# Four graph layers on one core: a comparison of the dilation on 2-byte operands in pairs of batches, and the second batch's transposes at the head of layer 2

## The chip, the core and the metric

The kernel runs on one core of one Trainium2 chip, as one program. The core has a matrix engine (TensorE, PE in the profile; its weight loads are listed apart as PEld), a vector engine (VectorE, DVE), a scalar engine (ScalarE, ACT), GpSimd (POOL) and a queue for transfers (SyncE, SP). Each engine works through its own list of instructions strictly in the order that the build gave it, and waits on semaphores for the others. The metric is the device time of one execution in microseconds (us); before the change the median of three runs is 2661.71 us.

## What is computed

Sixteen graphs of 1024 nodes with 128 features go through four layers; after each, the layer's output is added to its input and a layer norm is taken.

```python
x = _layernorm(x + _L0_gnn_ref(x, adj, ...))            # attention with a gate
x = _layernorm(x + _L1_gnn_ref(x, adj, nodemask, ...))  # dilation, then 3 x SAGE with batch norm
x = _layernorm(x + _L2_gnn_ref(x, adj, ...))            # attention, three gates
x = _layernorm(x + _L3_gnn_ref(x, adj, ...))            # GCN with the undilated adjacency
```

The dilation, which opens layer 1, runs over the rows of each graph's adjacency one after the other, and every row sees what the rows before it removed:

```python
row = jnp.take(carry, n, axis=0); nbi = row.astype(jnp.int32)
num = jnp.sum(nbi)
sf = jnp.where(num > T_DIL, (num + K_DIL - 1) // K_DIL, 1)
rank = jnp.cumsum(nbi)
rm = row & (rank % sf == 0)          # at most the middle and the last neighbour
carry = carry.at[n].set(row & ~rm); carry = carry.at[:, n].set(carry[:, n] & ~rm)
```

Layer 2 begins with the end of layer 1: `xc @ Wl + bl` on three hidden tensors, the residual and the layer norm. Then come `h = x W^T + b`, `G = A h`, and the attention, in which each score is the product of a row of `G` and a row of `h`.

## The kernel before, in words

The function `fast_kernel` builds the whole program. Tiles have 128 partitions; a graph is 8 x 8 blocks of 128 x 128. The loops are Python generators that are advanced in turns (`take_turns`, L811, `in_rounds`, L815, where a yielded number says how many rounds a stream pauses). From that program order a scheduler of the framework makes each engine's final list; an instruction marked with `keep_in_program_order` stays where the program put it.

**The dilation** (L1034 to L1193) handles a block of 128 rows k at a time, for two groups g of eight batches: 16 steps (k, g). Three generators share the work:

- `prepare` (L1047): for each half group of four batches, 32 products of `Y` blocks with step matrices make prefix counts `s0` in PSUM (L1068), and DVE multiplies them by the masked block into `sk`, float16, tile [128, 8 batches, 128] (L1070). For the last two blocks of rows (`with_last`) a tile `last` is made too (L1076).
- `fixed_point` (L1079): the rows of a block depend on each other, so the threshold of each row is found by iteration, `EVALS[k]` times (2, 3, 4, 7, 7, 3, 3, 9 for k = 0 to 7). One evaluation is: `thr = ti | 1` (L1091, int32, 8 numbers per partition), for the last two blocks `even` (L1094); the comparison `mid = (sk == thr)` over 1024 elements with an fp8 result (L1096); eight products of one column each that count `mid` into `pd` (L1099; with `last` eight more, L1101); and `ti = pd + v1m` (L1103). The final `mid` is removed from `Y` by xor (L1112), and a chain of small operations ends in `negc`, `posc` and `wid` (L1116 to L1129), which the removals of that step need. L1109 and L1112 read the final `mid` as 4-byte words, so it has to lie batch by batch.
- `removal` (L1132), once for each batch: 8 products (L1141, L1143), two ACT operations into `q` (L1144), on DVE `keep` (L1147) and an `and` into the rows (L1148), 9 products (L1151 to L1155), and one ACT operation that writes the columns back (L1156).

`take_turns` (L1180) lets the fixed point of step i alternate with the removals of step i - 1, among which the preparation of the same group's next block is spread. So one evaluation, one removal, and now and then half a preparation follow each other in DVE's list.

**The head of layer 2** is `before` (L1633) for batches 0 and 1 (L1819), ahead of all attention. For each batch GpSimd makes `yb`, the bias row times the node mask (L1639, one buffer); 24 products make `p` (L1644); DVE adds `yb` (L1660), adds the residual (L1664), and `normed` (L787) takes the layer norm, with its power on GpSimd (L745) and its last step on ACT (L801, eight pieces). `turned` (L754) transposes `xn` on PE (L759), ACT copies it to `xT` (L1669), and `products` (L762) with ACT copies makes `hT` (L1673) and `G` (L1677). `attention` (L1687) of batch 0 starts with a score product (L1706) and its masked minimum on DVE (L1711).

Of the kernel before, what the change touches and what calls it, by code (L numbers as in the profile page):

```python
# [10 lines left out]
F16 = mybir.dt.float16  # L11
F32R = mybir.dt.float32r
BF16 = mybir.dt.bfloat16
I32 = mybir.dt.int32
I8 = mybir.dt.int8
FP8 = mybir.dt.float8e4
AF = mybir.ActivationFunctionType
OP = mybir.AluOpType
# [4 lines left out]
P = 128  # L23
# [4 lines left out]
EVALS = 2, 3, 4, 7, 7, 3, 3, 9  # L28
GB = 8
QB = 4  # L30
# [609 lines left out]
def fast_kernel(ctx: ExitStack, tc: tile.TileContext, t: dict, out: bass.AP, flag: bass.AP):  # L640

    nc = tc.nc
    B, N, D = t["x"].shape
    NT = N // P
# [6 lines left out]
    identf = consts.tile([P, P], F32, name="identf")  # L651
# [18 lines left out]
    mf = consts.tile([P, BT], F32, name="mf")  # L670
# [57 lines left out]
    def tiles3(ap):  # L728
        return ap.rearrange("p (t d) -> p t d", d=P)

    def per_row(v):

        return v[:, :, None].to_broadcast([P, NT, P])

    def per_col(v):
        return v[:, None, :].to_broadcast([P, NT, P])
# [14 lines left out]
            p = psum.tile([P, 512], F32, name="ph", tag=tag)  # L751
            yield p, slice(h * 512, (h + 1) * 512), range(h * 4, h * 4 + 4)

    def turned(psum, src, tag="h"):  # L754

        for p, c, blocks in halves(psum, tag):
            for i, k in enumerate(blocks):
                s = src[:, k, :] if len(src.shape) == 3 else src[:, k * P:(k + 1) * P]
                nc.tensor.transpose(p[:, i * P:(i + 1) * P], s, identf)  # L759
            yield p, c, slice(blocks[0], blocks[-1] + 1)  # L760

    def products(psum, *pairs, tag="h"):  # L762
# [102 lines left out]
    onec = consts.tile([P, 1], BF16, name="onec")  # L865
# [26 lines left out]
    ps_h = ending.enter_context(tc.tile_pool(name="l0_ph", bufs=2, space=PSUM, reuse_waits="tile"))  # L892

    with tc.tile_pool(name="l0_raw", bufs=1, side="right") as raw:
# [4 lines left out]
        p = ps_h.tile([P, P], F32, name="wtr", tag="h")  # L899
# [3 lines left out]
        p = ps_h.tile([P, P], F32, name="wtr", tag="h")  # L903
# [3 lines left out]
        p = ps_h.tile([P, 1], F32, name="wtr", tag="h")  # L907
# [126 lines left out]
    with ExitStack() as ph:  # L1034
        sb = ph.enter_context(tc.tile_pool(name="dl_sb", bufs=2, side="right", reuse_waits="tile"))
        tiny = ph.enter_context(tc.tile_pool(name="dl_small", bufs=2, side="right", reuse_waits="tile"))
# [7 lines left out]
        def per_member(v):  # L1044
            return v[:, :, None].to_broadcast([P, v.shape[1], P])

        def prepare(st, k, g):  # L1047

            ks = slice(k * P, (k + 1) * P)
            st.with_last = k >= NT - 2  # L1050
            st.sk = sb.tile([P, GB, P], F16, name="sk")
            st.v1m = tiny.tile([P, GB], F32, name="v1m")
            st.l1 = tiny.tile([P, GB], F32, name="l1")
            if st.with_last:
                st.last = sb.tile([P, GB, P], FP8, name="last")
            for q in range(GB // QB):
                qs = slice(q * QB, q * QB + QB)
                b0 = g * GB + q * QB
                gs = slice(b0, b0 + QB)
                Yg = Yq[b0 // QB]  # L1060
                uY = sb.tile([P, QB, P], FP8, name="uY")
                nc.vector.tensor_tensor(words(uY), words(Yg[:, :, k, ks]),
                                        words(upper8)[:, None, :].to_broadcast([P, QB, P // 4]), op=OP.bitwise_and)
                s0 = ps_b.tile([P, QB, P], F32, name="s0")
                for i in range(QB):
                    for kb in range(NT):
                        m = step0 if kb == k else twos[:, :P if kb < k else 1]
                        nc.tensor.matmul(s0[:, i, :m.shape[1]], Y[b0 + i][:, kb, ks], m, start=(kb == 0), stop=(kb == NT - 1))  # L1068
                l1 = st.l1[:, qs]
                nc.vector.tensor_tensor(st.sk[:, qs, :], s0, uY, op=OP.mult)  # L1070
                nc.vector.scalar_tensor_tensor(l1, s0[:, :, 0], -1.0, off[:, k, gs], op0=OP.add, op1=OP.add)
                if not st.with_last:

                    nc.vector.tensor_tensor(past[:, k, gs], l1, s0[:, :, P - 1], op=OP.subtract)
                if st.with_last:
                    nc.vector.tensor_tensor(st.last[:, qs, :], st.sk[:, qs, :], per_member(l1), op=OP.is_equal, saturate=False)  # L1076
                yield

        def fixed_point(st, k, g):  # L1079

            ks = slice(k * P, (k + 1) * P)
            gs = slice(g * GB, (g + 1) * GB)
            st.negc = negc = tiny.tile([P, GB], F32, name="negc")
            st.wid = wid = tiny.tile([P, GB], F32, name="wid")
            v1m, l1 = st.v1m, st.l1
            nc.vector.tensor_scalar(v1m, l1, 0.5, -0.5, op0=OP.mult, op1=OP.add)
            ti = tiny.tile([P, GB], I32, name="ti")
            nc.vector.tensor_copy(ti, v1m)
            for e in range(EVALS[k]):
                thr = tiny.tile([P, GB], I32, name="thr")  # L1090
                nc.vector.tensor_scalar(thr, ti, 1, None, op0=OP.bitwise_or)  # L1091
                if st.with_last:
                    even = tiny.tile([P, GB], BF16, name="even")
                    nc.vector.tensor_tensor(even, thr, ti, op=OP.is_equal)  # L1094
                mid = sb.tile([P, GB, P], FP8, name="mid")
                nc.vector.tensor_tensor(mid, st.sk, per_member(thr), op=OP.is_equal, saturate=False)  # L1096
                pd = ps_d.tile([P, GB], F32, name="pd")
                for i in range(GB):
                    nc.tensor.matmul(pd[:, i:i + 1], mid[:, i, :], onec, start=True, stop=not st.with_last)  # L1099
                    if st.with_last:  # L1100
                        nc.tensor.matmul(pd[:, i:i + 1], st.last[:, i, :], even[:, i:i + 1], start=False, stop=True)  # L1101
                tn = tiny.tile([P, GB], I32, name="ti")
                nc.vector.tensor_tensor(tn, pd, v1m, op=OP.add)  # L1103
                prev, ti = ti, tn
                yield
            nc.vector.tensor_tensor(bad[:, 0, k, gs], ti, prev, op=OP.not_equal)
            if st.with_last:
                nc.vector.tensor_tensor(st.last, st.last, per_member(even), op=OP.mult, saturate=False)
                nc.vector.tensor_tensor(words(mid), words(mid), words(st.last), op=OP.bitwise_or)  # L1109
            for q in range(GB // QB):  # L1110
                yw = words(Yq[g * GB // QB + q][:, :, k, ks])
                nc.vector.tensor_tensor(yw, yw, words(mid[:, q * QB:(q + 1) * QB]), op=OP.bitwise_xor)  # L1112


            v = tiny.tile([P, GB], F32, name="v")
            nc.vector.tensor_sub(v, l1, ti)  # L1116
            hw = tiny.tile([P, GB], F32, name="hw")
            nc.vector.tensor_tensor(hw, thr, prev, op=OP.is_equal)
            nc.vector.tensor_sub(negc, hw, v)
            nc.vector.scalar_tensor_tensor(hw, v, 0.5, hw, op0=OP.mult, op1=OP.mult)  # L1120
            nc.vector.tensor_sub(negc, negc, hw)
            st.posc = posc = tiny.tile([P, GB], F32, name="posc")
            nc.vector.scalar_tensor_tensor(posc, v, 2.0, negc, op0=OP.mult, op1=OP.add)
            en = tiny.tile([P, GB], F32, name="en")
            mk = mok[:, g * GB * NT + k:(g + 1) * GB * NT:NT]
            nc.vector.scalar_tensor_tensor(en, v, 10.5, mk, op0=OP.is_gt, op1=OP.mult)
            nc.vector.tensor_tensor(bad[:, 1, k, gs], en, mk, op=OP.not_equal)
            nc.vector.scalar_tensor_tensor(hw, hw, 1.0, en, op0=OP.add, op1=OP.mult)
            nc.vector.tensor_scalar(wid, hw, -1.0, None, op0=OP.add)  # L1129
            yield  # L1130
# [127 lines left out]
    with ExitStack() as ph:  # L1258
# [6 lines left out]
        ps_h = ph.enter_context(tc.tile_pool(name="l1_ph", bufs=4, space=PSUM, reuse_waits="tile"))  # L1265
# [290 lines left out]
    with ExitStack() as ph:  # L1556
# [3 lines left out]
        ps_h = ph.enter_context(tc.tile_pool(name="l2_ph", bufs=2, space=PSUM, reuse_waits="tile"))  # L1560
# [72 lines left out]
        def before(s, b):  # L1633
# [2 lines left out]
                l2.load(s, b)  # L1636
            yield 2
            yb = rows("yT")
            nc.gpsimd.tensor_tensor(yb, per_row(mf[:, b * NT:(b + 1) * NT]), per_col(blrow), op=OP.mult)  # L1639

            def summed(p, blocks, ls):
                for i, j in enumerate(blocks):
# [13 lines left out]
            for p, blocks in turns:  # L1656
                if b >= 2:
                    summed(p, blocks, range(3))
                k = slice(blocks[0], blocks[-1] + 1)
                nc.vector.tensor_add(yn[:, k, :], tiles3(p), yb[:, k, :])  # L1660
            yield 2

            for k in spans(b < 2):
                nc.vector.tensor_add(s.xn[:, k, :], s.xn[:, k, :], yn[:, k, :])  # L1664
            normed(small, s.xn, b < 2)
            yield 6
            s.xT = wide("xT", 2)
            for p, c, _ in turned(ps_h, s.xn):
                nc.scalar.copy(s.xT[:, c], p)  # L1669
            yield 1  # L1670
            s.hT = wide("hT", 2)
# [210 lines left out]
```

## Time and profile before

| what | value |
|---|---|
| median of three runs | 2661.71 us (2660.23 to 2662.22) |
| the profiled execution: its own time | 2657.81 us |
| its span in the trace | 2656.1 us |
| mean granted TensorE clock | 0.984 |
| busy share of the span | PE 94%, PEld 69%, DVE 79%, ACT 74%, POOL 13% |
| first and last comparison of the dilation (L1096) | 622.0 and 963.8 us |
| removals of the last step (7, 1) | 968.4 to about 991 us |
| head of layer 2: last transfer of layer 1's `h2T` issued, first masked minimum of the attention | 1620.3 and 1659.6 us |
| 1700 to 2500 us (layers 2 and 3 in rounds) | PE busy 98 to 99% of each 100 us |

The profile is one execution. Start times are counted from the start of its span. In rows of groups, the number behind the bar is the total busy time in us, the next is the mean duration of one instruction in ns, then the idle time of the engine just before, and what ended it. In a table of windows each engine has its busy time in that stretch and in brackets its instructions; PEclk is the granted share of the full TensorE clock. In a timeline the first number is the start, the second the length in us, and what stands in square brackets is the engine's idle time ahead of that instruction with the instruction that ended it.

### The profile page before, as it was taken

The numbers are of one execution on the slowest core, as the hardware profiler recorded it, in microseconds if no ns is written. First come the engines' busy times: TensorE is split into PE (matmuls) and PEld (weight loads), VectorE is DVE, ScalarE is ACT, GpSimd is POOL, SyncE is SP. The second block draws the span as 40 slices with busy tenths as digits, with TensorE's granted clock in tenths as the row PEclk, the third lists the DMA queues.
The fourth block names the chain that finished last, engine by engine and source line by source line (L and its number), as shares of the span: only waits on it lengthen the run. The fifth ranks groups of instructions, "written<-read, shape, count | busy, mean of one in ns | idle before, by whom it ended". The sixth has DMA issues, their size and how long they took to land.

```text
span 2656.1 us, 44982 instructions
## 1 busy us (share of the span) xinstructions
PE 2509.0 (94%) x16580; PEld 1838.7 (69%) x16584; DVE 2106.4 (79%) x5832; ACT 1957.0 (74%) x3141; POOL 356.3 (13%) x316
## 2 busy tenths in 40 slices
PE   7999999997888869999999998999999999999987
PEld 5777777675666648888888896566666666666655
DVE  5888888887899877777788875777888787887786
ACT  7898898886888866667656534777777777777774
POOL 0001111013000001111122133011111111111001
PEclk9999999998999989999999998999999999999998
DMA  5555555530000052224467582111222111111100
GB/s 195 177 171 176 167 167 183 168 113 21 2 3 2 2 214 96 96 96 146 156 241 249 198 291 105 40 48 65 74 87 70 64 64 64 64 64 64 48 25 26
DMA packets 110103, 285.72 MB, mean 108 GB/s; under 512 B 12080, under 2 KB 53168, under 8 KB 102704
## 3 DMA queue, kind: packets, MB, share of 16 engines
q1 hardware_dynamic: 88832, 197.17, 22.1%
q0 software_dynamic: 21040, 85.57, 9.1%
q8 instruction: 133, 2.18, 0.3%
q14 instruction: 98, 0.80, 0.1%
HBM read 202.85 MB, written 79.82 MB: 106 GB/s over the span
## 4 chain that ended last, share of the span: by engine, by line
PE 53%; DVE 19%; ACT 13%; issue 5%; POOL 4%; DMA 2%; POOLq 0%; ACTq 0%; DVEq 0%; SPq 0%
PE acc L1306 9%; PE ph L1628 8%; PE acc L1694 6%; PE ph L1440 5%; PE ph L759 3%; PE ph L1644 3%; PE acc L973 2%; PE pmm L1706 2%; PE pmm L724 2%; PE ph L1615 2%; ACT em L985 2%; PE ph L766 2%; ACT xn L801 2%; DVE mid L1096 2%; DVE keep L1147 2%
## 5 line engine op out<-in xcount | busy, mean ns | idle before, releaser
L973 PEld LDWEIGHTS acc<-hs,em 128*128 128x128 f32 x2048 | 250.2, 193 | 38.2 <-issue 27.0
L973 PE MATMUL acc<-hs,em 128*128 128x128 f32 x2048 | 270.6, 280 | 0.9 <-DVE hs L989 0.7
L1694 PE MATMUL acc<-ex,hs 128*128 128x512 f32 x512 | 250.3, 599 | 6.2 <-DVE hs L1721 4.1
L724 PE MATMUL pmm<-xT,G 128*128 128x512 f32 x512 | 251.4, 604 | 1.4 <-DVE mx L983 0.7
L801 ACT ACTIVATE xn<-xn,ln_nb,ln_rstd 128x128 f32<-128x128 f32 x512 | 204.8, 480 | 55.3 <-DVE ln_nb L799 55.3
L1306 PE MATMUL acc<-a,hi 128*128 128x512 f32 x768 | 235.0, 398 | 3.0 <-ACT hi L1272 3.0
L1306 PE MATMUL acc<-a,lo 128*128 128x512 f32 x768 | 228.3, 392 | 3.1 <-DVE lo L1273 3.1
L745 POOL TENSOR_TENSOR ln_rstd<-ln_rstd,mhalf 128x8 f32<-128x8 f32 (+1 forms) x69 | 107.9, 1564 | 806.1 <-DVE ln_rstd L742 452.2
L1714 ACT ACTIVATE ex<-em,mn 128x1024 f32<-128x1024 f32 x128 | 146.6, 1145 | 89.2 <-DVE mn L1711 85.9
L983 DVE CUSTOM_DVE_ANT_0 em<-pmm,msk 128x1024 f32<-128x1024 f32 x128 | 155.9, 1218 | 35.5 <-PE pmm L724 33.2
L985 ACT ACTIVATE em<-em,mx 128x1024 f32<-128x1024 f32 x128 | 146.0, 1141 | 48.0 <-DVE mx L983 46.4
L1706 PE MATMUL pmm<-G,hT 128*128 128x512 f32 (+3 forms) x416 | 171.4, 520 | 0.1
L1306 PEld LDWEIGHTS acc<-a,lo 128*128 128x128 f32 x768 | 142.9, 188 | 34.0 <-DVE lo L1273 4.5
L1306 PEld LDWEIGHTS acc<-a,hi 128*128 128x128 f32 x768 | 140.7, 188 | 33.6 <-ACT hi L1272 3.7
L1156 ACT ACTIVATE carry<-pc,negone 128x1024 fp8e4<-128x1024 f32 x128 | 141.4, 1116 | 27.0 <-PE pc L1155 24.3
L1711 DVE CUSTOM_DVE_ANT_0 em<-pmm,msk 128x1024 f32<-128x1024 f32 x128 | 155.2, 1213 | 2.3 <-PE pmm L1708 0.6
L931 ACT ACTIVATE carry<-an 128x1024 fp8e4<-128x1024 f32 x128 | 134.1, 1049 | 24.5 <-DMA an<-in_adj 23.7
L980 ACT ACTIVATE msk<-carry,l0nbig 128x1024 bf16<-128x1024 fp8e4 x128 | 145.9, 1139 | 0.0
L1702 ACT ACTIVATE msk<-A,nbig 128x1024 bf16<-128x1024 fp8e4 x128 | 144.1, 1136 | 0.0
L1628 PE MATMUL ph<-A,hi 128*128 128x512 f32 x512 | 143.7, 422 | 0.2 <-ACT hi L1618 0.2
L1694 PEld LDWEIGHTS acc<-ex,hs 128*128 128x128 f32 x512 | 87.4, 189 | 78.6 <-issue 52.8
L1295 ACT CAST a<-carry 128x1024 fp32r<-128x1024 fp8e4 x96 | 98.9, 1047 | 43.4 <-PE acc L1306 43.2
(315 smaller groups left out, 6214.0 us busy)
## 6 DMA issues: line engine op xcount, KB each, us to landing
an<-in_adj SPq DMA_DIRECT2D x128, 512.0 KB, 4.1
adj_d<-carry POOLq DMA_DIRECT2D x16, 1024.0 KB, 4.6
A<-dil_d SPq DMA_DIRECT2D x16, 1024.0 KB, 6.0
rdeg<-rdeg_d SPq DMA_DIRECT2D x32, 512.0 KB, 4.6
A<-adj_d SPq DMA_DIRECT2D x16, 1024.0 KB, 4.8
ag_d<-ag POOLq DMA_DIRECT2D x24, 512.0 KB, 5.7
ag<-ag_d SPq DMA_DIRECT2D x24, 512.0 KB, 5.8
x_d<-xn POOLq DMA_DIRECT2D x16, 512.0 KB, 3.9
```

What stands on the lines that cost most here:

```text
L724: nc.tensor.matmul(p[:, h * 512:(h + 1) * 512], lhsT, rhs[:, h * 512:(h + 1) * 512], start=True, stop=True)
L801: nc.scalar.activation(r[:, k.start + i, :], r[:, k.start + i, :], AF.Identity, scale=rstd[:, i:i + 1], bias=nb[:, i:i + 1])
L973: nc.tensor.matmul(s.acc[:, c], em[:, c], hs, start=(jt == 0 and k % 4 == 0), stop=(jt == NT - 1 and k % 4 == 3))
L980: nc.scalar.activation(msk, Y[b][:, jt, :], AF.Identity, scale=-BIG, bias=nbig)
L983: nc.vector.tensor_tensor_reduce(em, e, msk, 1.0, 3.0e38, op0=OP.add, op1=OP.min, accum_out=mn)
L985: nc.scalar.activation(em, em, AF.Exp, scale=-1.0, bias=mn, accum_out=sm)
L1306: nc.tensor.matmul(acc, part[:, jt, :], pieces[h * NT // 2 + k][:, jt - 2 * k, :], start=(part is parts[0] and jt == 0), stop=(part is par ...
L1628: nc.tensor.matmul(p, part[:, jt, :], A[jt][:, c], start=(jt == 0 and i == 0), stop=(jt == NT - 1 and i == 1))
L1694: nc.tensor.matmul(s.acc[:, c], hs, ex[:, c], start=(jt == 0), stop=(jt == NT - 1))
L1706: nc.tensor.matmul(e[:, c], s.hT[:, js], s.G[:, c], start=True, stop=True)
L1711: nc.vector.tensor_tensor_reduce(row, e, msk, 1.0, 0.0, op0=OP.add, op1=OP.min, accum_out=mn)
L1714: nc.scalar.activation(ex, row, AF.Exp, scale=-1.0, bias=mn, accum_out=sm)
```

## The change

In the dilation the tile `sk` is stored with two batches interleaved: [128, 4 pairs, 128, 2]. All evaluations but the last of a step compare `sk` with an int16 threshold and write a bfloat16 tile `pairs` of the same interleaved form; the count products then load every second element of it as weights. The last evaluation still writes the fp8 tile `mid` batch by batch, and reads `sk` with a step of two elements. `thr` and `ti` are int16 in place of int32.

At the head of layer 2, batch 0 no longer has its `yb` made by GpSimd: eight DVE operations make mask times bias row plus the product. Batch 1 pauses 9 rounds in place of 6 ahead of its transposes, and the first of them is kept in program order.

```diff
             st.with_last = k >= NT - 2
-            st.sk = sb.tile([P, GB, P], F16, name="sk")
+            st.sk = sb.tile([P, GB // 2, P, 2], F16, name="sk")
...
-                nc.vector.tensor_tensor(st.sk[:, qs, :], s0, uY, op=OP.mult)
+                sk = members(st.sk[:, q * QB // 2:(q + 1) * QB // 2])
+                nc.vector.tensor_tensor(sk, in_pairs(s0), in_pairs(uY), op=OP.mult)
...
-            ti = tiny.tile([P, GB], I32, name="ti")
+            ti = tiny.tile([P, GB], I16, name="ti")
...
             for e in range(EVALS[k]):
-                thr = tiny.tile([P, GB], I32, name="thr")
+                ends = e == EVALS[k] - 1
+                thr = tiny.tile([P, GB], I16, name="thr")
...
-                mid = sb.tile([P, GB, P], FP8, name="mid")
-                nc.vector.tensor_tensor(mid, st.sk, per_member(thr), op=OP.is_equal, saturate=False)
+                if ends:
+                    mid = sb.tile([P, GB, P], FP8, name="mid", bufs=1)
+                    nc.vector.tensor_tensor(in_pairs(mid), members(st.sk), in_pairs(per_member(thr)), op=OP.is_equal, saturate=False)
+                    picked = [mid[:, i, :] for i in range(GB)]
+                else:
+                    pairs = sb.tile([P, GB // 2, P, 2], BF16, name="pairs")
+                    nc.vector.tensor_tensor(pairs, st.sk, thr.rearrange("p (a c) -> p a c", c=2)[:, :, None, :].to_broadcast([P, GB // 2, P, 2]),
+                                            op=OP.is_equal)
+                    picked = [pairs[:, i // 2, :, i % 2] for i in range(GB)]
...
-                    nc.tensor.matmul(pd[:, i:i + 1], mid[:, i, :], onec, start=True, stop=not st.with_last)
+                    nc.tensor.matmul(pd[:, i:i + 1], picked[i], onec, start=True, stop=not st.with_last)
...
-            nc.gpsimd.tensor_tensor(yb, per_row(mf[:, b * NT:(b + 1) * NT]), per_col(blrow), op=OP.mult)
+            if b:
+                nc.gpsimd.tensor_tensor(yb, per_row(mf[:, b * NT:(b + 1) * NT]), per_col(blrow), op=OP.mult)
...
-                nc.vector.tensor_add(yn[:, k, :], tiles3(p), yb[:, k, :])
+                if b:
+                    nc.vector.tensor_add(yn[:, k, :], tiles3(p), yb[:, k, :])
+                else:
+                    for i, j in enumerate(blocks):
+                        nc.vector.scalar_tensor_tensor(yn[:, j, :], blrow, mf[:, j:j + 1], p[:, i * P:(i + 1) * P],
+                                                       op0=OP.mult, op1=OP.add)
...
-            yield 6
+            yield 9 if b == 1 else 6
             s.xT = wide("xT", 2)
-            for p, c, _ in turned(ps_h, s.xn):
+            for p, c, _ in turned(ps_h, s.xn, behind=b == 1):
```

The two helpers are views: `in_pairs` splits the batches into pairs, `members` moves the inner pair index ahead of the elements. In `turned`, `behind` marks the first transpose:

```diff
+                turn = nc.tensor.transpose(p[:, i * P:(i + 1) * P], s, identf)
+                if behind and k == 0:
+                    tc.keep_in_program_order(turn)
```

In the built lists of instructions, PE's order at the head changes from 16 transposes of `xn` (both batches), then 4 products with `W2T`, to 8 transposes and the products of batch 0 (`hT`, `G`), its transposes of `hT` with the first two score products between them, and only then batch 1's 8 transposes. ACT's order there becomes: batch 0's `xT` and `hT`, the first half of its `G`, all eight norm pieces of batch 1, the second half of batch 0's `G`. From the middle of batch 0's attention on, PE's list is the same as before. In the dilation the lists of all engines differ in places, and where layer 1 begins SP issues two loads of `n` ahead of the fourth load of `A` (L1369).

More of the change, by code (lines that the diff above doesn't have):

```diff
@@ L14 @@
 I32 = mybir.dt.int32
+I16 = mybir.dt.int16
 I8 = mybir.dt.int8
@@ L752, in halves, with turned @@
             yield p, slice(h * 512, (h + 1) * 512), range(h * 4, h * 4 + 4)
-    def turned(psum, src, tag="h"):
+    def turned(psum, src, tag="h", behind=False):
         for p, c, blocks in halves(psum, tag):
@@ L758, in turned @@
                 s = src[:, k, :] if len(src.shape) == 3 else src[:, k * P:(k + 1) * P]
-                nc.tensor.transpose(p[:, i * P:(i + 1) * P], s, identf)
+                turn = nc.tensor.transpose(p[:, i * P:(i + 1) * P], s, identf)
+                if behind and k == 0:
+                    tc.keep_in_program_order(turn)
             yield p, c, slice(blocks[0], blocks[-1] + 1)
@@ L1045, in per_member, with in_pairs, members @@
             return v[:, :, None].to_broadcast([P, v.shape[1], P])
+        def in_pairs(v):
+            return v.rearrange("p (a c) d -> p a c d", c=2)
+        def members(v):
+            return v.rearrange("p a d c -> p a c d")
         def prepare(st, k, g):
@@ L1075, in prepare @@
                 if st.with_last:
-                    nc.vector.tensor_tensor(st.last[:, qs, :], st.sk[:, qs, :], per_member(l1), op=OP.is_equal, saturate=False)
+                    nc.vector.tensor_tensor(in_pairs(st.last[:, qs, :]), sk, in_pairs(per_member(l1)), op=OP.is_equal, saturate=False)
                 yield
@@ L1094, in fixed_point @@
                     nc.vector.tensor_tensor(even, thr, ti, op=OP.is_equal)
-                mid = sb.tile([P, GB, P], FP8, name="mid")
-                nc.vector.tensor_tensor(mid, st.sk, per_member(thr), op=OP.is_equal, saturate=False)
+                if ends:
[7 more added lines that the diff above has]
+                    picked = [pairs[:, i // 2, :, i % 2] for i in range(GB)]
                 pd = ps_d.tile([P, GB], F32, name="pd")
                 for i in range(GB):
-                    nc.tensor.matmul(pd[:, i:i + 1], mid[:, i, :], onec, start=True, stop=not st.with_last)
+                    nc.tensor.matmul(pd[:, i:i + 1], picked[i], onec, start=True, stop=not st.with_last)
                     if st.with_last:
                         nc.tensor.matmul(pd[:, i:i + 1], st.last[:, i, :], even[:, i:i + 1], start=False, stop=True)
-                tn = tiny.tile([P, GB], I32, name="ti")
+                tn = tiny.tile([P, GB], I16, name="ti")
                 nc.vector.tensor_tensor(tn, pd, v1m, op=OP.add)
```

## The prediction, made before the changed kernel was run

> **What bounds the kernel now.** I read the page first: slices, then groups.
>
> ```profile
> PE   7999999997888869999999998999999999999987
> DVE  5888888887899877777788875777888787887786
> PEclk9999999998999989999999998999999999999998
> ```
>
> PE has 9 tenths or more nearly everywhere, with two dips that the change touches: slices 11 to 15 (the dilation; a slice is 66.4 us), where DVE has as much as PE, and slice 25, the head of layer 2. In both the end is set by something else than PE's work.
>
> For the dilation I cut the trace into its steps, from the first `q` of one step's removals to that of the next. Columns: PE, PEld, DVE, ACT, POOL busy, granted clock, DMA.
>
> ```profile
> 714.87:735.38 20.51, 18.57 (x237) 13.59 (x236) 18.26 (x53) 18.00 (x25) 0.00 (x0) 1.00 0.01 2
> 735.38:759.28 23.90, 20.05 (x272) 14.56 (x272) 22.15 (x61) 19.38 (x27) 0.00 (x0) 1.00 0.02 4
> 781.13:802.95 21.82, 19.13 (x256) 13.99 (x256) 21.25 (x61) 18.06 (x25) 0.00 (x0) 1.00 0.01 2
> 842.53:862.81 20.28, 18.51 (x227) 13.85 (x226) 17.15 (x51) 18.17 (x26) 0.00 (x0) 1.00 0.01 2
> 907.10:939.57 32.47, 22.96 (x356) 17.83 (x356) 29.84 (x82) 19.47 (x25) 0.00 (x0) 0.88 0.00 1
> 939.57:968.38 28.81, 21.09 (x281) 14.70 (x281) 24.77 (x68) 18.55 (x25) 4.32 (x8) 0.86 0.72 289
> ```
>
> Rows 1 and 4 hold 4 and 3 evaluations: no engine is full, and the step takes about 20.4 us. Rows 2 and 3 are two of the four steps with 7 evaluations: DVE is at 93 and 97%. The last two hold 9 each: 32.5 and 28.8 us, with ACT idle for a third. ACT's timeline says for what:
>
> ```profile
> 939.57 0.69 ACT L1144 ACTIVATE q<-s,negc 128x512 f16<-128x512 f32 x1 [8.72 <-DVE negc L1121]
> 968.38 0.69 ACT L1144 ACTIVATE q<-s,negc 128x512 f16<-128x512 f32 x1 [5.28 <-DVE negc L1121]
> ```
>
> The removals of block 7 wait 8.72 and 5.28 us for the end of their fixed point. Then the groups of which the change is made:
>
> ```profile
> L1147 DVE TENSOR_SCALAR keep<-q,wid 128x1024 fp8e4<-128x1024 f16 x128 | 95.5, 748 | 30.9 <-ACT q L1144 30.4
> L1096 DVE TENSOR_TENSOR mid<-sk,thr 128x1024 fp8e4<-128x1024 f16 x76 | 92.7, 1219 | 0.7
> L1070 DVE TENSOR_TENSOR sk<-s,uY 128x512 f16<-128x512 f32 x32 | 22.0, 687 | 12.4 <-PE s L1068 12.4
> L973 PEld LDWEIGHTS acc<-hs,em 128*128 128x128 f32 x2048 | 250.2, 193 | 38.2 <-issue 27.0
> L1099 PEld LDWEIGHTS <-mid 128*128 128x128 fp8e4 x608 | 25.7, 96 | 35.0 <-DVE mid L1096 32.9
> L1151 PEld LDWEIGHTS <-identb 128*128 128x128 bf16 x128 | 12.5, 98 | 7.5 <-DVE carry L1148 2.2 <-issue 1.4
> ```
>
> For the head, PE's timeline and the clock:
>
> ```profile
> 1642.60 1.63 PE L759 MATMUL ph<-identf,xn 128*128 128x128 f32 x4 [5.21 <-ACT xn L801]
> 1644.71 1.63 PE L759 MATMUL ph<-identf,xn 128*128 128x128 f32 x4 [0.48 <-ACT xn L801]
> 1646.33 6.35 PE L766 MATMUL ph<-xT,l2WT 128*128 128x512 f32 x8
> ```
>
> ```profile
> 1636.00:1642.00 6.00, 1.23 (x4) 0.46 (x4) 5.27 (x17) 2.02 (x5) 3.22 (x2) 0.67 0.33 122
> 1646.00:1650.00 4.00, 4.00 (x6) 1.60 (x7) 0.00 (x0) 1.55 (x3) 0.00 (x0) 0.50 0.01 2
> ```
>
> ACT copies batch 0's `xT` from 1636.92 to 1638.02, but its products start at 1646.33, since PE's list has batch 1's transposes first and these wait for batch 1's layer norm. Over that idle time the clock falls to 0.50, and the next 5 us run at half speed.
>
> **The comparison.** 60 of the 76 comparisons become 2-byte throughout; the 16 last ones stay. At two elements per tick 1024 elements cost what 512 do now: 687 ns (L1070), so 0.53 us less each, 32 us of DVE in all. That two-source DVE instructions do two elements per tick, no row of before shows; the one-source `keep` does better than one (748 ns for 1024 against 1219). [...] Bounds: 0.69 and 1.22; I take 0.69.
>
> What of the 32 us lies on the path, by kind of step (evaluations that shrink: all but the last):
> - Block 0 (2 x 1): under GpSimd's 20 us power and the layer norm that waits for it. Nothing.
> - 7 evaluations (four steps, 735.38 to 824.47, 89.1 us): 24 x 0.53 = 12.8 us off the full DVE. Next late are ACT and the chain of one removal, as in the steps with 3 or 4 evaluations: 20.57, 20.51, 20.28 and 21.09, mean 20.6. So 82.4: 6.7 us.
> - 9 evaluations (block 7): one evaluation beside a removal is now `even` 0.17, `mid` 1.14, `keep` 0.66, `ti` 0.15, `carry` 0.33, `thr` 0.11 of DVE without a gap, 2.56 us. With 0.53 less it is 2.03, but a removal needs 2.18 of ACT (the last step's alone run at that beat, 983.63 to 985.81), so 0.38 x 16 = 6.1; the first evaluations wait for the preparation anyway. I take 5.5.
> - 3 or 4 evaluations (18 that shrink, 9.6 us): DVE is at 75 to 89%; about a sixth on the path, 1.5.
>
> Sum 13.7, rounded to 13.5. Bounds: 6 (half of what the full steps give) and 18 (the chain of waits holds some 42 of the 76; four fifths of them times 0.53). It moves the start of layer 1 by as much, and nothing takes it back: from 1030 us PE is full.
>
> What else moves: `sk` is written, and by the last evaluation read, at a step of 4 bytes. That is adjacent words, as every f32 row has, and L1443 writes 512 f32 in 682 ns: nothing, at worst 0.3 us x 32 on DVE, some 5 us on the path. `thr`, `ti` as int16: 8 numbers, 0.16 us either way. One `mid` buffer: its next writer comes a step later. The weights of the count products become bf16 at a step of 4 bytes, 480 loads: a dense bf16 load takes 98 ns, fp8 96, f32 193. [...] With no such row in the trace, the bounds are 98 and 193. The two `n` loads that SP issues ahead of the fourth `A` are not waited for in the trace: nothing.
>
> **The head.** Batch 0's yT (1.9 us of GpSimd) goes; its `yn` waits for PE's `py` (1626.5) anyway, and eight small DVE operations in place of two add about 0.5. Batch 1's yT then runs at 1624.2 instead of beside batch 0's two residual adds, which took 1.49 each where such an add takes 0.69: 1.6 back. So `xT` comes about 1.1 earlier, at 1637, PE is still at full clock, and `hT` and half of `G` are done by 1641. Then a new wait: ACT has the second half of `G` behind batch 1's eight norm pieces, which end near 1645.3; the second score product and all behind it on PE, batch 1's transposes first, start at about 1645.9. Behind them, at 0.86 per 512-wide product and 0.44 per four transposes (the chain's pieces): 5 to 6 products and 20 to 24 transposes of preparation and two more score products, 8.2 us. The idle time from 1641.5 to 1645.9 costs clock again as above, 5 us at half speed, 2.5. All that is done at 1656.6; before, the same state comes at 1660.0 + 2 x 0.86 = 1661.7. Gain 5. Bounds: 7.6 (clock stays), 2 (batch 1 is later, or the idle time longer). Behind it PE's list is the same and PE is 98% busy to 2500 us, so it lasts.
>
> **Sum.** 13.5 + 5 = 18.5 us off the profiled execution's own 2657.8, so 2639.3; the median of the runs is 3.9 above it: 2643.
>
> **The rivals.**
> - *One element per tick.* The mixed f16, i16 and bf16 operands, or the repeated pair, keep the DVE at 1219 ns. For it: no row of before shows the fast two-source form. Then only the head's 5 us: 2657.
> [...]
> - *The strided weights cost an f32 load* (slower). 95 ns more x 8 is 0.76 us of PE per shrunk evaluation, more than the 0.53 that DVE saves. In a 7-evaluation step PE goes from 19.1 to 23.7 us and becomes the bound, some 2 us above today's 21.8: +8; in block 7 the evaluation's chain grows by 0.23 x 16: +4; in the other steps 1 us each: +8. With the head's 5 back: +15, 2677. It decides from about 67 ns per load on. Against: the dense bf16 load is no slower than fp8.
> - *The head gives nothing*, because batch 1's norm holds everything behind it: 2648.
>
> **How the numbers follow.** As forecast 0.66; head gives nothing 0.07; hopping rate 0.07; one per tick 0.11; slow weights 0.09. 0.2% is 5.3 us, about what a measurement of this kernel can tell from no change. Faster: 0.66 + 0.07 + 0.07 = 0.80; the one-per-tick case falls within: 0.11; slower 0.09. The range: 2633 (19 and 8 gained, and 1.7 for what else is shorter) to 2657 (one per tick); the slow weights are left out.
>
> **What would show it.** L1096's successors with bf16 output at 0.69 us x60, and 1.22 x16; their weight loads near 98 ns; 7-evaluation steps near 20.6 us with DVE below 90%; ACT's two waits of 8.72 and 5.28 us for `negc` shortened by about 2.5 each; the dilation's end some 13 us earlier; batch 0's first products with `W2T` near 1637 minus that, the second half of `G` behind batch 1's norm. Wrong, if loads are above 165 ns, if steps stay at 21.8 with DVE idle, or if the head's saved time reappears as PE's idle time ahead of batch 1's transposes.

## The result and the profile after

| | before | after |
|---|---|---|
| median of 6 runs each | 2661.41 us (2657.59 to 2664.31) | 2635.93 us (2633.43 to 2641.83) |
| profiled execution: own time, span | 2657.81, 2656.1 | 2634.23, 2632.1 |
| mean granted clock | 0.984 | 0.987 |

The ratio after to before is 0.9906, 95% interval 0.9896 to 0.9916: 25 us less (22.4 to 27.7). Forecast were 18.5 us less (2643, range 2633 to 2657): 6.5 us of the gain were not foreseen. The span of the profiled execution is 24.0 us shorter, 5.5 more than forecast.

The page's slices after the change (66 us each), for PE and DVE:

```profile
PE   7999999997999979999999998999999999999987
DVE  5888888887888867777788876678877878877886
```

The dip of PE in slices 11 to 15 is mostly gone, one 7 is left in slice 15, where block 7 runs, and no slice of DVE there is a 9 any more. The dip of PE at the head of layer 2, slice 25, is an 8 still.

The same six steps of the dilation, cut from first `q` to first `q` as before (PE, PEld, DVE, ACT, POOL, clock, DMA):

```profile
713.11:732.83 19.72, 18.00 (x233) 13.23 (x233) 15.78 (x51) 17.98 (x25) 0.00 (x0) 1.00 0.01 2
732.83:754.27 21.44, 19.45 (x272) 14.36 (x272) 19.46 (x61) 18.13 (x25) 0.00 (x0) 1.00 0.01 2
774.57:795.06 20.49, 18.98 (x267) 14.34 (x266) 18.60 (x61) 17.88 (x25) 0.00 (x0) 1.00 0.01 2
835.71:855.89 20.18, 18.31 (x227) 13.64 (x226) 16.27 (x51) 18.02 (x24) 0.00 (x0) 1.00 0.01 2
897.78:923.43 25.65, 22.62 (x357) 17.51 (x356) 24.21 (x77) 19.35 (x27) 0.00 (x0) 0.99 0.01 2
923.43:947.10 23.67, 19.57 (x282) 13.69 (x281) 21.34 (x71) 18.15 (x25) 4.31 (x8) 0.93 0.69 279
```

Rows 2 and 3 (7 evaluations) went from 23.90 and 21.82 to 21.44 and 20.49 us, DVE in them from 93 and 97% to 91%: now these steps are as long as those with few evaluations. Rows 5 and 6 (block 7) went from 61.28 to 49.32 us together. ACT's two waits for `negc`, 8.72 and 5.28 us before, are 5.87 and 2.37 us shorter (forecast were about 2.5 each). Its timeline after:

```profile
923.43 0.69 ACT L1164 ACTIVATE q<-s,negc 128x512 f16<-128x512 f32 x1 [2.85 <-DVE negc L1141]
947.10 0.69 ACT L1164 ACTIVATE q<-s,negc 128x512 f16<-128x512 f32 x1 [2.91 <-DVE negc L1141]
```

And the groups that the change is made of, in the table of lines with shapes apart:

```profile
L1114 DVE TENSOR_TENSOR pairs<-sk,thr 128x1024 bf16<-128x1024 f16 x60 | 41.2, 687 | 0.6
L1110 DVE TENSOR_TENSOR mid<-sk,thr 128x1024 fp8e4<-128x1024 f16 x16 | 19.5, 1222 | 0.2
L1119 PEld LDWEIGHTS <-pairs 128*128 128x128 bf16 x480 | 20.0, 97 | 14.5 <-DVE pairs L1114 12.4
L1082 DVE TENSOR_TENSOR sk<-s,uY 128x512 f16<-128x512 f32 x32 | 23.4, 730 | 15.3 <-PE s L1079 15.0
```

The comparison takes 687 ns against 1222 for the 16 that stayed, the strided bf16 weights load in 97 ns. The write of `sk` at a step of two elements takes 730 ns where it took 687.

Laid out by markers of the two traces, the 24.0 us come from here. The steps' lengths, in order of k and g, from the second row of blocks on: k = 1 and 2 give 3.7 us, the four with 7 evaluations 6.7, k = 5 and 6 nothing (0.1), block 7 12.0. Together 22.5, of which 1.2 are taken off because the dilation itself started 1.2 later. From the first `q` of step (7, 1) to the bias row of layer 2 (`l2A`, L1240 before and L1260 after) the time is the same (655.5 and 655.8). From there to masked minimum number 4 of the attention: 44.8 before, 40.9 after, 3.9 us gained. From masked minimum number 4 to the end: 987.4 and 988.2, 0.8 lost. 21.3 - 0.3 + 3.9 - 0.8 = 24.1, the 24.0 of the spans but for rounding. I take number 4 since the earlier ones mislead: in this measure the first is 7.9 us earlier and the third only 2.1, and from the fourth on all keep one distance, 24.7 to 24.8 us, for the next 600 us.

PE's and ACT's timeline at the head after, and two windows of it:

```profile
1617.05 1.98 PE L769 MATMUL ph<-xT,l2WT 128*128 128x512 f32 x4 [0.24 <-ACT xT L1695]
...
1625.65 0.68 PE L760 MATMUL ph<-identf,hT 128*128 128x128 f32 x4 [2.51 <-DVE hn L1706]
...
1626.45 0.57 ACT L1703 ACTIVATE G<-ph 128x512 f32<-128x512 f32 x1
```

```profile
1622.00:1626.00 4.00, 1.49 (x6) 0.54 (x5) 1.67 (x9) 2.75 (x7) 1.57 (x2) 1.00 0.00 0
1626.00:1630.00 4.00, 3.25 (x13) 2.47 (x12) 0.69 (x1) 2.20 (x5) 0.00 (x0) 0.52 0.00 0
```

Batch 0's products with `W2T` no longer wait for batch 1. PE then runs dry, as forecast: it has 1.49 us of work in 4, and the clock is 0.52 in the next 4 us. The first and longer wait, 2.51 us, the trace puts down to `hn`, DVE's copy of the first half of batch 0's transposed `hT`. It starts at 1624.90, right behind the second `ln_nb` of batch 1's norm in DVE's list, which had waited 1.18 us for GpSimd. The forecast wait for the second half of `G`, evicted at 1626.45 behind batch 1's eight norm pieces, ends last and adds 0.75 us.

### The profile page after: what moved, and what is told of

It reads as the page before. It is cut to its first block, busy times and chain, and to the rows that moved or that the text cites. A ratio compares the mean times of both kernels' runs of the same rounds, so it can differ in the third digit from the quotient of the medians.

```text
span 2632.1 us, 44972 instructions
## 1 busy us (share of the span) xinstructions
PE 2503.9 (95%) x16584; PEld 1836.2 (70%) x16584; DVE 2078.7 (79%) x5838; ACT 1954.6 (74%) x3141; POOL 353.7 (13%) x315
## 3 DMA queue, kind: packets, MB, share of 16 engines
q1 hardware_dynamic: 88832, 197.17, 22.6%
q8 instruction: 133, 2.18, 0.3%
## 4 chain that ended last, share of the span: by engine, by line
PE 49%; DVE 19%; ACT 15%; issue 6%; POOL 4%; DMA 4%; POOLq 0%; ACTq 0%; DVEq 0%; SPq 0%
PE acc L1326 9%; PE ph L1648 8%; PE acc L1720 6%; PE ph L1460 4%; PE ph L1665 3%; ACT em L988 3%; PE ph L760 3%; ACT xn L804 2%; PE pmm L1732 2%; DMA an<-in_adj 2%; PE ph L1635 2%; PE ph L769 2%; ACT msk L983 2%; POOL ln_rstd L746 2%; DVE keep L1167 2%
## 5 line engine op out<-in xcount | busy, mean ns | idle before, releaser
L976 PEld LDWEIGHTS acc<-hs,em 128*128 128x128 f32 x2048 | 250.2, 193 | 37.8 <-issue 27.2
L1737 DVE CUSTOM_DVE_ANT_0 em<-pmm,msk 128x1024 f32<-128x1024 f32 x128 | 155.4, 1214 | 10.1 <-PE pmm L1732 7.1
L934 ACT ACTIVATE carry<-an 128x1024 fp8e4<-128x1024 f32 x128 | 134.1, 1049 | 27.4 <-DMA an<-in_adj 26.4
```

The source lines that it names most:

```text
L976: nc.tensor.matmul(s.acc[:, c], em[:, c], hs, start=(jt == 0 and k % 4 == 0), stop=(jt == NT - 1 and k % 4 == 3))
L1737: nc.vector.tensor_tensor_reduce(row, e, msk, 1.0, 0.0, op0=OP.add, op1=OP.min, accum_out=mn)
```

## The experiments

The two theories at the start. *A*: the gain is the comparison's rate, and block 7 gives 12 us of it, since a shrunk evaluation returns its full 0.53 us and waits with it; the head gives 4 to 5. *B*: the prediction's sizes hold, ACT's removal sets block 7's beat, and what is more than forecast comes from the head or from the rebuilt lists. All times are compared with runs of the kernel before on the same chip; the bracket is the 95% interval, in us from the ratio times the median of before.

**1. The dilation alone.** `before` at the head is as in the kernel before (both edits undone).

```diff
-            if b:
-                nc.gpsimd.tensor_tensor(yb, ...)
+            nc.gpsimd.tensor_tensor(yb, ...)
...
-            yield 9 if b == 1 else 6
+            yield 6
```

> Dilation part alone, head of layer 2 as before. Theory A (from the two traces: the first score's inputs of layer 2 come 21.0 us earlier, 12.0 of it in the two steps of block 7): -21 us against the kernel before, 2640.4; the steps of block 7 take 25.7 and 23.7 us as in the changed kernel. Theory B (the sizes of the prediction, the rest of the result from the head): -13.5 us, 2648.

2639.55 against 2663.21, ratio 0.9915 (0.9901 to 0.9928): -22.6 us (-26.4 to -19.2). A; 13.5 lies outside the interval. In its trace the steps from k = 1 on have the lengths of the changed kernel within 0.03 us, except the last, 24.80 (23.67); the part on block 7 below says why that one varies.

**2. The head alone.** The dilation is that of before, the head that of the changed kernel.

```diff
-                    pairs = sb.tile([P, GB // 2, P, 2], BF16, name="pairs")
...
+                mid = sb.tile([P, GB, P], FP8, name="mid")
+                nc.vector.tensor_tensor(mid, st.sk, per_member(thr), op=OP.is_equal, saturate=False)
```

> Head part alone, dilation as before. Theory A (masked minimum number 4 of the attention and all after it come 3.8 us earlier than the dilation explains): -3.8 us, 2657.6. Theory B (the early first masked minimum is what counts): -8 us, 2653.5. Theory C (head gives nothing, the new wait takes it all): within 0.5 us of before, 2661.

2656.27, ratio 0.998 (0.997 to 0.9989): -5.3 us (-8.0 to -2.9). C is out, A and B both lie in the interval. The trace decides: masked minimum number 4 comes 40.4 us after the bias row, against 44.8 before, so 4.4, not 8. With run 1 the parts add up to 27.9, for a whole of 25.0; the intervals cover that.

**3. One operand of 4 bytes.** `thr` and `ti` are int32 again; layout, bf16, strided weights and head stay in the program.

```diff
-            ti = tiny.tile([P, GB], I16, name="ti")
+            ti = tiny.tile([P, GB], I32, name="ti")
...
-                thr = tiny.tile([P, GB], I16, name="thr")
+                thr = tiny.tile([P, GB], I32, name="thr")
```

> Everything as in the changed kernel (pair layout, bf16 result, strided weights, head), but thr and ti are int32 again, so one operand has 4 bytes. Theory A (the gain is the rate): comparisons at 1.22 us, the dilation's 21 us are gone, head's 3.8 stay, and the strided write of sk costs up to 32 x 0.043 = 1.4 on DVE: 2657 to 2659. Theory B (layout, bf16 weights or the new order of the lists bring part of it): 2640 to 2650. If the mixed sizes do not lower the rate: 0.69 us and 2636.

2657.01, ratio 0.9977 (0.9968 to 0.9986): -6.1 us (-8.5 to -3.7), the head's gain and no more. Its groups:

```profile
L1114 DVE TENSOR_TENSOR pairs<-sk,thr 128x1024 bf16<-128x1024 f16 x60 | 73.2, 1221 | 0.5
```

All steps from k = 1 on have the lengths of before within 0.1 us (block 7: 32.50 and 28.78). So 8 numbers of 4 bytes undo the whole gain of the dilation, and the strided loads and the slower write of `sk` cost nothing that can be seen while DVE is slow.

Not only the rate went back, though. The scheduler's order did too: in the trace DVE's order is that of before in 13 of the 15 steps, and ACT's in all 15 (in run 4 both are, in all 15). The run tells the rate and the order that comes with it from the layout, but not the one from the other. Only in step (2, 0) do DVE and ACT have the same order before and after the change; there 20.57 us became 19.30, 1.27 of the 1.59 (3 x 0.53) that DVE saves. So the rate pays without a new order of these two lists; how much of the rest the new order brings is open.

**4. 2-byte, but batch by batch.** `sk`, the result and the weights are dense, and `thr`, int16, is repeated element by element.

```diff
-            st.sk = sb.tile([P, GB // 2, P, 2], F16, name="sk")
+            st.sk = sb.tile([P, GB, P], F16, name="sk")
...
-                    nc.vector.tensor_tensor(pairs, st.sk, thr.rearrange("p (a c) -> p a c", c=2)[:, :, None, :].to_broadcast([P, GB // 2, P, 2]),
-                                            op=OP.is_equal)
-                    picked = [pairs[:, i // 2, :, i % 2] for i in range(GB)]
+                    nc.vector.tensor_tensor(pairs, st.sk, per_member(thr), op=OP.is_equal)
+                    picked = [pairs[:, i, :] for i in range(GB)]
```

> 2-byte operands throughout, but batch by batch: sk, the bf16 result and the weights are dense, thr is int16 and each element repeats one 2-byte number 128 times. [...] Theory B (the operand size alone decides): comparisons at 0.69 us, sk's write back at 687 ns, 2634 to 2636.

2657.30, ratio 0.9977 (0.9968 to 0.9986): -6.1 us (-8.5 to -3.7). B is out, the comparisons take 1220 ns and not 0.69 us:

```profile
L1114 DVE TENSOR_TENSOR pairs<-sk,thr 128x1024 bf16<-128x1024 f16 x60 | 73.2, 1220 | 0.6
L1082 DVE TENSOR_TENSOR sk<-s,uY 128x512 f16<-128x512 f32 x32 | 22.0, 688 | 11.5 <-PE s L1079 11.5
```

2-byte operands alone are not enough here: with the pair the comparison took 687 ns, with the number repeated singly 1220. The second line shows that it is the stride of the write, and nothing else of the change, that makes `sk` 730 instead of 688.

**5 and 6. Where the rate is worth what.** The comparison in pairs only in block 7, and only elsewhere. The diff is that of the first; the second has `k < NT - 1`. The other evaluations read the same `sk`, and write fp8 batch by batch into the same buffer, at 1.22 us.

```diff
+                elif not (k == NT - 1):
+                    raw = sb.tile([P, GB // 2, P, 2], BF16, name="pairs")
+                    pairs = raw[:, :GB // 4].rearrange("p a d c -> p (a d c)").bitcast(FP8).rearrange("p (i d) -> p i d", d=P)
+                    nc.vector.tensor_tensor(in_pairs(pairs), members(st.sk), in_pairs(per_member(thr)), op=OP.is_equal, saturate=False)
+                    picked = [pairs[:, i, :] for i in range(GB)]
```

> Changed kernel, but the comparison in pairs only in block 7 (16 of 60); the other evaluations compare the same sk into fp8, batch by batch, at 1.22 us. Theory A (block 7's evaluations follow one another at DVE's own beat, so each gives back its whole 0.53 us and the waits of ti for the counts shrink too: 12 us as the steps of the two traces say; head 4 to 5): -16 to -17 us against before. Theory B (the prediction's size, ACT's beat of a removal holds block 7 to 5.5): -10 us.

> The complement: pairs in blocks 0 to 6 (44 of 60), block 7 at 1.22 us. Theory A: 6.7 from the 7-evaluation steps, 2.4 from the others, head 4 to 5: -13 to -14 us against before; with the run that has block 7 alone it adds up to the whole, the head counted once. Theory B (block 7 is worth 5.5, the rest more): -19 us.

Block 7 alone: 2646.34 against 2662.07, ratio 0.9942 (0.9929 to 0.9955), -15.4 us (-18.9 to -12.0). All but block 7: 2647.34, 0.995 (0.9937 to 0.9963), -13.3 us (-16.8 to -9.9). In both A, and B's number is outside the interval. By the steps of the traces (k = 1 on) the first gives 9.9, the second 11.5, both together 22.5; some 1 us comes only with both. Block 7 is thus worth 10 to 12, about half of the dilation's gain for 16 of the 60 comparisons.

**7. Is ACT tied to an evaluation?** The first half of `q` is computed twice in the removals beside block 7's evaluations.

```diff
+                if h == 0 and (k, g) in ((NT - 2, 1), (NT - 1, 0)):
+                    nc.scalar.activation(q[:, :512], s, AF.Abs, scale=1.0, bias=st.negc[:, i:i + 1])
```

> Changed kernel with one more ACT operation of 0.57 to 0.69 us in every removal that lies beside block 7's evaluations (the first half of q is computed twice in steps 6,1 and 7,0): 16 in all, 9 to 11 us of ACT. Theory A (ACT is not tied to one evaluation, and has 5 to 7 us of slack in each of the two steps): at most 2 us slower than the changed kernel, -23 to -25 against before. Theory B (a removal's time on ACT sets the evaluation's beat, as the prediction had it): the beat goes from 2.18 to 2.8 us, 9 us slower than the changed kernel, -16 against before.

2641.38 (2632.04 to 2643.5), ratio 0.9919 (0.9903 to 0.9934): -21.6 us (-25.8 to -17.6); the interval holds A's number and also 5.8 us more than the changed kernel, what the trace gives; B's -16 lies just outside it. The trace: the two steps grow from 25.65 to 28.64 and from 23.67 to 26.48 us, 2.9 each. Neither theory: A had at most 1 each, B 4.5. The evaluations themselves hardly slow down, from 2.10 and 2.22 us apart to 2.22 and 2.28; most of the growth is behind the last one, until ACT is through with the removals. ACT's timeline at the end of the first of the two steps:

```profile
926.89 1.11 ACT L1178 ACTIVATE carry<-pc,negone 128x1024 fp8e4<-128x1024 f32 x1 [1.43 <-DVE negc L1139]
927.90 0.68 ACT L1165 ACTIVATE q<-s,negc 128x512 f16<-128x512 f32 x1
```

The first `q` of the next step no longer waits for `negc`, it follows the last removal's `carry` at once; so it does at the end of the second. So ACT has a limit over the whole step, not over an evaluation, and its slack there was the 2.85 and 2.91 us of the two waits: 8 x 0.69 = 5.5 more, less 2.9, is 2.6, near the 2.9 seen.

**8 to 10. The head, taken apart.** Three versions beside a repeat of the changed kernel on one chip: without the pin and with 6 rounds of pause; with batch 0's `yb` back on GpSimd; and one meant to be better, in which batch 1's norm comes later in the program.

```diff
-            yield 9 if b == 1 else 6
+            yield 6
...
-            for p, c, _ in turned(ps_h, s.xn, behind=b == 1):
+            for p, c, _ in turned(ps_h, s.xn):
```

```diff
-                if b:
-                    nc.vector.tensor_add(yn[:, k, :], tiles3(p), yb[:, k, :])
-                else:
...
+                nc.vector.tensor_add(yn[:, k, :], tiles3(p), yb[:, k, :])
```

```diff
-            yield 2
+            yield 10 if b == 1 else 2

             for k in spans(b < 2):
...
-            yield 9 if b == 1 else 6
+            yield 2 if b == 1 else 6
```

> The changed kernel once more, on the chip of the three runs beside it, so that they can be told from it: -22 to -28 us against before.

> Changed kernel without the pin and with 6 rounds of pause for batch 1: PE's list has 16 transposes of xn ahead of the products again; batch 0's bias stays on DVE. In the runs with the head changed, masked minimum number 4 comes 37.8 to 40.9 us after the first bias row is ready (mean 39.7), with the old head 44.6 to 44.8. Theory A (the order on PE is what counts): 43 to 44.5 in this measure, 4 to 5 us slower than the changed kernel. [...]

> Changed kernel with batch 0's yb on GpSimd and added as before, the pin kept. Theory A (the order counts): batch 1's residual adds come some 1 us later, masked minimum number 4 at 40 to 41.5 us after the bias row, within 1.5 us of the changed kernel. Theory B (the bias counts): 44 and 4 us slower.

> Changed kernel, but batch 1 pauses 10 rounds in place of 2 ahead of its residual and 2 in place of 9 ahead of its transposes. In ACT's list the second half of batch 0's G then stands behind one of batch 1's eight norm pieces, not behind all; from the fifth score on all lists are as in the changed kernel. Theory A (that wait and the lower clock behind it still cost some of the head): second score product about 3 us earlier, 1 to 3 us faster than the changed kernel, -26 to -28 against before. Theory B (batch 1's norm holds what follows anyway): no difference, -25.

> The version with batch 1's pauses at 10 and 2 again, now beside the changed kernel on one chip. If the second half of G behind batch 1's norm pieces costs anything: 37.5 us in the measure above, 1 to 3 us faster than the changed kernel. Otherwise the same within 1 us.

| version | median, us | ratio to before | less, us | bias row to masked minimum 4, us |
|---|---|---|---|---|
| changed kernel, repeated | 2636.71 | 0.9909 (0.9895 to 0.9922) | 24.2 (20.8 to 27.9) | 40.0 |
| no pin | 2643.60 | 0.9931 (0.9917 to 0.9945) | 18.4 (14.6 to 22.1) | 47.1 |
| bias on GpSimd | 2634.59 | 0.9897 (0.9882 to 0.9913) | 27.4 (23.1 to 31.4) | 39.4 |
| later norm, first time | 2633.22 | 0.9907 (0.9892 to 0.9921) | 24.8 (21.0 to 28.8) | 37.5 |
| later norm, again | 2638.74 | 0.9914 (0.99 to 0.9927) | 22.9 (19.4 to 26.6) | 37.9 |

The order on PE is what counts: without the pin the head's gain is gone (47.1 is even above the 44.6 to 44.8 of the old head; PE waits 6.5 us for batch 1's norm there, and its clock was 0.90 from 1577.85 to 1610.85 us, where the changed kernel had 1.00 from 1574.10 to 1607.10). The bias moved to DVE is worth nothing that can be seen: without it the version is not slower, and the measure is 39.4. The measure holds two waits of PE for loads of layer 1's `h`, in sum 2.2 to 3.6 us over these traces (2.2 in that of before, 2.9 in that of the changed kernel), so a difference of 1 us in it says little.

The later norm does in the trace what it was made for. ACT has the second half of `G` behind one norm piece, the other seven follow it (its timeline at that place, then two windows), and PE's clock stays whole:

```profile
1620.25 0.49 ACT L804 ACTIVATE xn<-xn,ln_nb,ln_rstd 128x128 f32<-128x128 f32 x1 [2.08 <-DVE ln_nb L802]
1620.65 0.58 ACT L1703 ACTIVATE G<-ph 128x512 f32<-128x512 f32 x1
```

```profile
1620.00:1624.00 4.00, 1.55 (x9) 1.11 (x10) 2.27 (x10) 3.75 (x10) 1.03 (x2) 1.00 0.00 0
1624.00:1628.00 4.00, 4.00 (x14) 2.06 (x13) 1.55 (x3) 2.54 (x6) 0.00 (x0) 1.00 0.01 4
```

Masked minimum number 4 comes about 2 us earlier than on average in the eight traces with the whole new head and the norm where it was (37.8 to 40.9, mean 39.8; one of them is as early). But the times of whole runs do not show it: once 24.8 us less, once 22.9, beside 25.0 and 24.2 of the changed kernel. So no version was shown to beat the changed kernel; a gain of 2 us is smaller than these runs can tell.

## Why the prediction was nearly right, step by step

- *The rate.* Taken as 0.69 us, measured 0.687. No row of before showed a two-source instruction at that rate; 0.69 was the author's estimate, from the 687 ns that 512 elements took. No run shows what the forecast's chances call the hopping rate: the comparison took 687 ns as forecast, and in the other forms that were run it was as slow as before. What the runs add is how narrow the fast form is: 1221 ns with one 4-byte operand (run 3), 1220 with 2-byte numbers repeated singly (run 4). Run 3 gives up the 2-byte numbers, run 4 the pair, and each loses all of the gain.
- *Strided weights* 98 ns forecast, 97 measured. No row of before showed a strided load; that it would take the 98 ns of a dense one was the author's estimate. The rival that would have made the kernel slower falls.
- *Steps with 7 evaluations.* 6.7 us forecast, 6.7 measured. Here the sum set the steps' own measured length, 22.3 on average, against the length of the steps that DVE does not bound. DVE is at 91% in the two of them shown; below 90 was forecast.
- *Block 7.* The term that failed: 5.5 forecast, 12.0 by the pair of traces, 10 to 12 by runs 5 and 6. The prediction put an evaluation "without a gap" at 2.56 us before and at ACT's 2.18 after. The value after was good: the 16 distances between comparisons are 2.16 on average in the changed trace (2.10 and 2.22 by step). The value before was not: in the trace of before those distances are 2.79 and 3.00 in the two steps, 2.90 on average. 0.74 x 16 = 11.8. The gap-free evaluation is the best of them, not the typical one, and the waits that I left out shrank as well. Nor did ACT become the bound: in the two rows of block 7 DVE is busy for 94 and 90% of the time after the change (92 and 86% before), ACT for 75 and 77%. DVE's waits in both steps, before and after:

```profile
DVE ti L1103 <- PE pd L1101: 5.1, 9, 1.4
```

```profile
DVE ti L1123 <- PE pd L1121: 1.9, 4, 0.8
```

  In all 5.1 us before, in 9 waits, and 1.9 after, in 4: 3.2 less, beside 16 x 0.53 = 8.5 of work, 11.7 together. Where they shrank, the traces show. 1.9 of the 3.2 lie at the last two evaluations of each step: before, the removals were through by then, at most one operation of 0.16 us stood between the comparison and `ti` in DVE's list, and DVE waited 0.60, 0.61, 0.65 and 0.57 us for the counts; after, one such wait is left, 0.57. Another 1.0 is the wait of the second evaluation of step (7, 1), 1.35 before and 0.31 after. It goes with the TensorE clock, in executions whose DVE and ACT lists are the same: of the seven traces with the changed dilation, three have 0.31 us at a clock of 0.84 to 0.85 (in the 5 us that begin 1.5 us into the step), three 1.30 to 1.41 at 0.59 to 0.61, and one 2.03 at 0.50; in the trace of before the clock is 0.59. The row of the changed kernel, then that of run 9:

```profile
924.93:929.93 5.00, 4.99 (x69) 3.64 (x68) 3.82 (x13) 3.67 (x6) 0.19 (x1) 0.85 0.00 0
```

```profile
924.49:929.49 5.00, 5.00 (x41) 3.39 (x40) 3.39 (x9) 2.30 (x4) 0.00 (x0) 0.50 0.00 0
```

  The last step is 23.67 or 23.68 us long in three of the seven traces and 24.68 to 25.50 in the others, so block 7 gives 10.1 to 12.0 us, 11.2 on average; the pair shown above is at the upper end. Whether the removals no longer end ahead of the evaluations because of the rate, or because of the rebuilt lists, was not tried apart: where block 7 compares at 1.22 us the distances of before return (in run 3 2.85, 3.35 and 3.41 are among them), but in run 3 DVE and ACT have the order of before there too. That ACT's 2.18 was close to the outcome is no proof of the reason given for it: in run 7 ACT's removals grew to some 2.9 us and the evaluations only to 2.25.
- *Steps with 3 or 4 evaluations.* 1.5 forecast, 3.8 measured (3.7 of it in k = 1 and 2).
- *`sk`.* "Nothing, at worst 0.3": 0.043 us each, 1.4 of DVE; not visible in the steps of run 3. No run shows the 0.3, which was the author's guess.
- *The head.* 5 forecast; 3.9 in the pair of traces, 4.9 as the mean over eight, 5.3 (2.9 to 8.0) by its own run. A new wait behind batch 1's norm (2.51 and 0.75 us) and the lower clock (0.52) came as described, though the longer part of the wait ended with DVE's `hn` and not with ACT's `G`. The part on the bias ("1.6 back", 1.1 us earlier) bought nothing that run 9 could find, and the trace says why. Batch 0's two residual adds take 1.29 us together, where they took 2.98, and its eight small operations 2.16, where two took 1.29: 0.8 earlier. But `xT` starts 13.5 us after the bias row, 13.1 before: the transposes ahead of it, which used to wait for the norm, now wait until PE is through with batch 1's `py` products at 1615.8, and these had waited 2.12 and 0.79 us for their loads of layer 1's `h`.

18.5 was forecast, and the terms above sum to 12.0 + 6.7 + 3.8 + 3.9 = 26.4 in the traces, less 1.2 of the later start, 0.3 and 0.8 behind: 24.1. Block 7 was forecast 6.5 too small and the steps with few evaluations 2.3; that the head fell 1.1 short in this pair, and that 2.3 were lost elsewhere, brought the whole nearer to the forecast than its terms, which is luck.

## What to carry to other kernels

Cost a step from its own measured length against the length at which the next engine stops it, not from its best repetition: the gaps between repetitions are part of the chain, and they can shrink together with the work, as block 7's did from 5.1 to 1.9 us. An engine that trails a loop may be bound by the sum over the whole loop and not by each turn; its idle time at the loop's end is the slack. For a two-source DVE comparison of 2-byte data against one number per partition and batch, interleave two batches, so that the broadcast operand is a repeated pair of 2-byte numbers: for 1024 elements it took 687 ns here, where the singly repeated number took 1220 and a pair of 4-byte numbers 1221.

## What the runs showed of the hardware beside that

- The DVE multiply from PSUM into the f16 `sk` took 688 ns for 512 elements into adjacent 2-byte places (run 4) and 730 into every second one (the changed kernel).
- The bf16 weight loads from every second element took 97 ns in the changed kernel, the dense fp8 loads of `mid` 96.
- Single executions of one list differ by some 6 us in layer 1, where the granted clock differs: from the first `q` of step (7, 1) to the bias row 655.8 us in the changed kernel, 661.6 without the pin, whose lists are the same there. Its clock is 0.83 against 0.90 in the first 33 us of that stretch, and 0.95 against 1.00 in the 33 us that begin 363 us later. Differences of 2 us in the sum of a run can't be read from one profile.
- At the head PE was idle for 2.5 us in one piece and busy for 1.5 of 4, and the clock was 0.52 in the next 4 us. In the version with the later norm PE had 1.55 of 4 in pieces with at most 1.54 of idle time ahead of one, and the clock stayed at 1.00.
